# Shared experts of the first half of the tokens beside the second half's scan, and the first half's MLP at twice the pace

## The chip, the cores and the metric

The kernel runs on one core of one Trainium2 chip. The metric is the device time of one execution in microseconds (us). The number that counts is the median of several executions.

## The reference, cut to what matters

One layer for 512 tokens of width 512, in three parts, each added to `x`:

```python
x = x + xattn(layernorm(x), ctx)          # 16 heads, 8192 context rows
u = layernorm(x)
u = u + ssm(rmsnorm(u))                    # mamba: conv, selective scan, gate, out_proj
x = x + u + mlp(rmsnorm(u))                # silu(h w1) * (h w3), times w2; hidden 2048
u = layernorm(x)
logits = u @ router_w                      # 16 experts, top 2, sigmoid gates
moe = sum over the 2 chosen experts of gate * (silu(u wg) * (u wu)) wd      # hidden 512
shared = (silu(u sg) * (u su)) sd          # shared experts, hidden 1024
x = x + moe + shared
```

The scan is `h[t] = exp(delta[t] A) h[t-1] + delta[t] B[t] x[t]` for 1024 channels with 16 states each, and `y[t] = sum over states of C[t] h[t]`.

## The kernel before, in words

Every product of matrices is made in three fp16 products of high and low halves. A framework records the program in the order of the Python code, and a scheduler then puts each engine's instructions into one fixed order; each engine works through its own queue strictly in that order. What the code calls earlier has the higher priority. All loads and stores discussed here are issued from SP's queue.

The attention takes the first 1760 us or so. The tail (function `tail`) does the rest, in two halves of 256 tokens, `s` = 0 and 1:

- `prep(s)` makes the in-projection, convolution and the inputs of the scan. `delta(s, q)` makes the step sizes of a quarter of the channels and the gate input `zs` (products `pd` and `pz`).
- `scan(s, b)` does a block of 128 channels; each quarter `q` has two blocks `b`. A block has four steps of four states. A step is, on ACT, four exponentials into `dA` (L909); on DVE, a product into `hs` (L912), the scan itself (L916) and a product with C (L919); on PE, four fp32 matmuls that add the states up in `py` (L922). There are three buffers `dA` and three `hs`, used in turn. For `s` = 1, ACT also copies the carried states into `hs` (L911). `gate(s, q)` multiplies by `zs` (L928 to L930).
- `outproj(s)` makes the output projection (`px`), updates `u_sb` and makes the normed input `h2` of the MLP.
- `ffn(s, h2, names, pm)` is a generator. It does a gated two-layer product in blocks of 256 hidden channels: 8 blocks for the MLP, 4 for the shared experts. A block loads three pieces of weights of 512 KB into `wpm` (five buffers, L761), makes `pg` and `pu` with 24 matmuls each (L703 to L705), then SiLU on ACT (L966, which needs another activation table than the exponentials), a product on DVE (L967), the fp16 halves `gg` on ACT and DVE (L969, L970), yields, and then does the 12 matmuls of the down product (L709 to L711) into two accumulators. At its end the accumulators are added to `x_sb` on DVE (L978), and it yields once more.
- `ln2(s, xT, fill)` is the norm before the experts with its transposes (L686, L690, L691) and the router products (L1008). It calls `fill` twice, to put other work between.

The quarters of both halves follow each other in one loop (`seq`). From the first block of half 1 on, the loop holds `ml`, the MLP of half 0, and calls it once after the first block of a quarter and once after the second. After the loop come the last gate, `outproj(1)` with one call of `ml`, and the rest of `ml`. Then the buffers of the recurrence are given back (`M.close()`); the expert weights use that space. The MLP of half 1 follows, with `ln2(0)` called inside it; then the shared experts of half 0 (`rs0`) with `ln2(1)` inside; then the choice of experts (top 2, ranks by small products `prk`, slot numbers `sg`), eight indirect DMAs on POOL that scatter the token rows to their experts (L1201), the rest of `rs0`, and the shared experts of half 1. Last, `moe` goes through 16 experts and two spare slots: it gathers the rows of an expert (`xd`, L1208), transposes them, and makes the expert's products. Each expert's weights come in six pieces of 512 KB (`wef`, six buffers, L1089), are split into halves on ACT and DVE (L1094, L1095) and go into `we` (18 buffers) or `wpm`.

Of the kernel before, what the change touches and what calls it, by code (L numbers as in the profile page):

```python
# [632 lines left out]
def tail(tc, a, out, const, scr, ident, x_sb, mlp_d, oT, y_d, xd_d, psums):  # L633
# [16 lines left out]
    def acc(i):  # L650
        if i < 2:
            return ps_s.tile([P, DM], F32, name=f"acc{i}", tag="pss")
        nacc[0] += 1
        if nacc[0] % 3 == 0:
            return ps_o.tile([P, DM], F32, name="acc3", tag="po0")
        return ps_x.tile([P, DM], F32, name="acc4", tag="px")
# [4 lines left out]
    def rsqrt(out_, t, n, tag):  # L661
        nc.scalar.activation(out_, t, AF.Ln)
        nc.scalar.activation(out_, out_, AF.Exp, scale=-0.5)
        w = T.tile([P, n], F32, name=f"nw_{tag}", tag=f"nwt{n}", bufs=2)
        nc.vector.tensor_mul(w, out_, out_)
        nc.vector.tensor_mul(w, w, t)
        nc.vector.tensor_scalar(w, w, -0.5, 1.5, ALU.mult, ALU.add)
        nc.vector.tensor_mul(out_, out_, w)

    def stats(src, n, tag):  # L670
        st = T.tile([P, n, 6], F32, name=f"st_{tag}", tag=f"st{n}", bufs=2)
        mv = T.tile([P, n, 2], F32, name=f"mv_{tag}", tag=f"mv{n}", bufs=2)
        for i in range(n):
            nc.vector.bn_stats(st[:, i, :], src[:, i, :])
            nc.vector.bn_aggr(mv[:, i, :], st[:, i, :])
        return mv

    def small(n, name):
        return T.tile([P, n], F32, name=name, tag=f"sm{n}", bufs=6)
# [20 lines left out]
    def mm_block(ps, w, j, xh, xl, first=True):  # L700
        wr = w.rearrange("p x (b d m) -> p x b d m", b=2, d=NC4)
        for i in range(NC4):
            nc.tensor.matmul(ps, lhsT=wr[:, 0, j, i, :], rhs=xh[:, i, :], start=i == 0, stop=False)  # L703
            nc.tensor.matmul(ps, lhsT=wr[:, 0, j, i, :], rhs=xl[:, i, :], start=False, stop=False)
            nc.tensor.matmul(ps, lhsT=wr[:, 1, j, i, :], rhs=xh[:, i, :], start=False, stop=i == NC4 - 1)  # L705

    def mm_down(ps, xh, xl, w, j, start, stop):
        wh, wl = w[:, 0, j * 512 : j * 512 + 512], w[:, 1, j * 512 : j * 512 + 512]
        nc.tensor.matmul(ps, lhsT=xh, rhs=wh, start=start, stop=False)  # L709
        nc.tensor.matmul(ps, lhsT=xh, rhs=wl, start=False, stop=False)  # L710
        nc.tensor.matmul(ps, lhsT=xl, rhs=wh, start=False, stop=stop)  # L711
# [47 lines left out]
    def wload(n, i):  # L759
        w = F.tile([P, 2, 1024], F16, name="wpm", tag="wpm", bufs=5)  # L760
        nc.sync.dma_start(w, mlp_d[n][i])  # L761
        return w
# [96 lines left out]
    def load_bc(s, k, pool_):  # L859
        bf = bc_d[s].rearrange("(o n) t -> o (n t)", o=1)  # L860
        for nq in range(4):
            x = pool_.tile([P, 4, H], F32, name=f"bc{k}{nq}")
            o = (k * 16 + nq * 4) * H
            nc.sync.dma_start(x.rearrange("p n t -> p (n t)"), bf[:, o : o + 4 * H].to_broadcast((P, 4 * H)))
            BC[s][k, nq] = x
# [59 lines left out]
    def gate(s, q, yT):  # L925
        dl, du, zs, py = dlu.pop((s, q))
        y = m2.tile([P, 2, H], F32, name="y", tag="w2k", bufs=5)
        nc.vector.tensor_mul(y, py, zs)  # L928
        nc.scalar.copy(yT[:, 0, 2 * q : 2 * q + 2, :], y)
        nc.vector.tensor_tensor(yT[:, 1, 2 * q : 2 * q + 2, :], y, yT[:, 0, 2 * q : 2 * q + 2, :], ALU.subtract)  # L930
# [24 lines left out]
    def ffn(s, h2, names, pm):  # L955
        nf = len(mlp_d[names[0]])
        for f2 in range(nf):
            wg, wu, wd = (wload(n, f2) for n in names)
            pg = bank_j([P, 2, H], F32, "pg")
            pu = bank_j([P, 2, H], F32, "pu")  # L960
            for j in range(2):
                mm_block(pg[:, j, :], wg, j, h2[:, 0], h2[:, 1])
            for j in range(2):
                mm_block(pu[:, j, :], wu, j, h2[:, 0], h2[:, 1])
            g = F2.tile([P, 2, H], F32, name="g32", bufs=2)
            nc.scalar.activation(g, pg, AF.Silu, scale=IW)  # L966
            nc.vector.scalar_tensor_tensor(g, pu, IW, g, ALU.mult, ALU.mult)  # L967
            gg = F2.tile([P, 2, 2, H], F16, name="gg", bufs=2)
            nc.scalar.copy(gg[:, 0], g)  # L969
            nc.vector.tensor_tensor(gg[:, 1], g, gg[:, 0], ALU.subtract)  # L970
            yield
            for i in range(2):
                sl = slice(i * P, (i + 1) * P)
                for j in range(2):
                    k = 2 * f2 + j
                    mm_down(pm[i], gg[:, 0, j, sl], gg[:, 1, j, sl], wd, j, k == 0, k == 2 * nf - 1)
        for i in range(2):
            nc.vector.scalar_tensor_tensor(x_sb[:, 2 * s + i], pm[i], IW, x_sb[:, 2 * s + i], ALU.mult, ALU.add)  # L978
        yield
# [5 lines left out]
    nc.vector.scalar_tensor_tensor(rw[:, 1], rwf, WF, rw[:, 0], ALU.mult, ALU.subtract)  # L985
    lg = T.tile([P, 4, 16], F32, name="lg")

    def ln2(s, xT, fill=lambda: None):
        ts_ = slice(2 * s, 2 * s + 2)
        mv = stats(x_sb[:, ts_, :], 2, f"l2{s}")  # L990
        v, r = small(2, f"lv{s}"), small(2, f"lr{s}")
        nc.vector.tensor_scalar(v, mv[:, :, 1], 1e-5, None, ALU.add)
        rsqrt(r, v, 2, f"d{s}")
        h = u_sb[:, ts_]
        for i in range(2):
            nc.vector.tensor_scalar(
                h[:, i], x_sb[:, 2 * s + i], mv[:, i, 0:1], r[:, i : i + 1], ALU.subtract, ALU.mult
            )
        fill()
        transposeT(h, xT[:, 0], xT[:, 1])  # L1000
        fill()
        pl = bank_j([P, 2, 16], F32, "plg")
        for i in range(2):
            sl = slice(i * P, (i + 1) * P)
            n = 0
            for d in range(NC4):
                for x, y in ((0, 0), (0, 1), (1, 0)):
                    nc.tensor.matmul(  # L1008
                        pl[:, i, :], lhsT=xT[:, x, d, sl], rhs=rw[:, y, d, :], start=n == 0, stop=n == 11
                    )  # L1010
                    n += 1
        nc.scalar.activation(lg[:, ts_, :], pl, AF.Copy, scale=IW)

    MLP, RS = ("w1", "w3", "w2"), ("rsg", "rsu", "rsd")

    def h2tile():
        return F2.tile([P, 2, NC4, H], F16, name="h2", bufs=2)
# [27 lines left out]
    h2s = [h2tile() for _ in range(2)]  # L1045
# [2 lines left out]
    xin[1] = const.tile([P, 2, 8, H], F32, name="xin1", tag="big16")[:, 0]  # L1048
    p1 = prep(1)
    yTs = [m3.tile([P, 2, 8, H], F16, name="yT", bufs=2)]  # L1050
    seq = [(s, q) for s in range(2) for q in range(4)]
    ml = None
    for i, (s, q) in enumerate(seq):
        scan(s, 2 * q)
        if s == 0:
            next(p1, None)
        if i:
            gate(*seq[i - 1], yTs[-1])
        if (s, q) == (1, 0):
            outproj(0, yTs[-1], h2s[0])  # L1060
            ml = ffn(0, h2s[0], MLP, [acc(3), acc(3)])
            yTs.append(m3.tile([P, 2, 8, H], F16, name="yT", bufs=2))
        if ml and (s, q) != (1, 0):
            next(ml, None)
        if i + 1 < len(seq):
            if (s, q) == (0, 3):
                for _ in p1:
                    pass
                load_bc(1, 1, m3)
            delta(*seq[i + 1])  # L1070
        scan(s, 2 * q + 1)
        if s == 0:
            next(p1, None)
        if ml:
            next(ml, None)
    gate(1, 3, yTs[-1])
    outproj(1, yTs[-1], h2s[1], lambda: next(ml, None))
    for _ in ml:
        pass
    M.close()  # L1080

    G, g2 = pool(es, "G", "left"), pool(es, "g2", "left")
# [33 lines left out]
    one16 = G.tile([P, 16], F32, name="one16")  # L1116
    nc.gpsimd.memset(one16, 1.0)

    mlp1 = ffn(1, h2s[1], MLP, [acc(0), acc(1)])
    next(mlp1)  # L1120
    xT0 = h2tile()
    ln2(0, xT0, lambda: next(mlp1))
    for _ in mlp1:
        pass
    xT1 = h2tile()
    rs0 = ffn(0, xT0, RS, [acc(3), acc(3)])
    ln2(1, xT1, lambda: next(rs0, None))
    xf = const.tile([P, 4, 2, DM], F16, name="xf", tag="big16")
    nc.scalar.copy(xf[:, :, 0, :], u_sb)
    nc.vector.tensor_tensor(xf[:, :, 1, :], u_sb, xf[:, :, 0, :], ALU.subtract)  # L1130
# [15 lines left out]
        )  # L1146
    oht = G.tile([P, 4, 16], F16, name="oht")
    nc.vector.tensor_add(oht, oh[:, 0], oh[:, 1])
    next(rs0, None)
    prk = bank_j([P, 5, 16], F32, "prk")  # L1150
    for i in range(5):
        n = min(i, 4)
# [118 lines left out]
        moe_down(prev[0], moe_turn(prev[1]), prev[2])  # L1271

    regs = [nc.sync.value_load(oii[0:1, k : k + 1], min_val=0, max_val=15) for k in range(NOV)]
    for _ in rs0:
        pass
    for _ in ffn(1, xT1, RS, [acc(3), acc(3)]):
        pass
    moe(range(16 + MOV), lambda k: expert(k) if k < 16 else overflow(regs[k - 16]))
    total = nc.values_load(oii[0:1, NOV : NOV + 1], min_val=0, max_val=NOV)
# [82 lines left out]
```

## Time and profile before

| | us |
|---|---|
| median of 3 runs | 2606.5 |
| lowest and highest | 2605.04 and 2607.05 |
| profiled execution, its own time | 2611.01 |
| its span, first to last instruction | 2609.3 |
| PE busy | 2383.2 (91%) |
| DVE busy | 2062.4 (79%) |
| ACT busy | 1949.2 (75%) |
| mean DMA rate over the span | 204 GB/s |
| first MLP matmul of half 0 (in the profiled execution) | 2093.2 |
| last L919 of half 1's scan | starts at 2220.3 |
| last expert matmul of the first product (L1225) | starts at 2575.5 |

The profile is of one execution. The table of busy times is an average over very different stages, so the text works with windows of the span, in us from its start. "PEclk" is the granted share of the TensorE clock, "PEld" the loading of weights into the array, "SPq" the queue from which DMAs are issued. A row of waits names the engine and line that waited and what ended its wait. A matmul's duration in a row is longer than the distance to the next one's start, because matmuls overlap.

### The profile page before, as it was taken

Reading aid. Unit: us, or ns where it says so; the run is one execution under the profiler, and the core shown is the slowest. Engines: PE = TensorE matmul, PEld = TensorE weight load, DVE = VectorE, ACT = ScalarE, POOL = GpSimd, SP = SyncE. Lnnn points to the kernel's source line nnn. Section 1 sums busy time; section 2 is a strip of 40 time slices with the busy share of each in tenths; the row PEclk is TensorE's granted clock in tenths of the full one; section 3 lists DMA queues with packets and bytes.
Section 4 is the critical chain, followed back from the end, with each engine's and each line's share of the span. In section 5 each row is a group of like instructions: output and inputs, shape, how many; then the busy total and the mean of one; then the engine's idle time right before and its main releaser. Section 6 shows DMA issues by size and latency. Waiting matters only on the chain. (4 is left out here: it accounts for less than half of the span.)

```text
span 2609.3 us, 54424 instructions
## 1 busy us (share of the span) xinstructions
PE 2383.2 (91%) x21806; PEld 1676.5 (64%) x21806; DVE 2062.4 (79%) x2403; ACT 1949.2 (75%) x3734; POOL 44.3 (2%) x58
## 2 busy tenths in 40 slices
PE   7999899999999999999999998997877688998895
PEld 3555577776677777767777777995665466665442
DVE  6776588888888888878888778997899999533785
ACT  5787788888788888868888888997776476333784
POOL 2000000000000000000000000000000000001001
PEclk9999999999999999999999999999989899999998
DMA  7974677778687778778877655877510222766896
GB/s 270 312 259 138 231 212 231 229 235 241 199 234 235 226 221 251 226 199 228 236 221 213 175 156 148 207 205 192 159 41 25 97 81 82 260 225 217 293 331 208
DMA packets 353688, 531.43 MB, mean 204 GB/s; under 512 B 25107, under 2 KB 218835, under 8 KB 353301
## 3 DMA queue, kind: packets, MB, share of 16 engines
q1 hardware_dynamic: 352148, 523.69, 65.8%
q0 software_dynamic: 1280, 4.20, 0.5%
q8 instruction: 173, 2.83, 0.5%
q14 instruction: 87, 0.70, 0.1%
HBM read 397.68 MB, written 126.94 MB: 201 GB/s over the span
## 5 line engine op out<-in xcount | busy, mean ns | idle before, releaser
L377 DVE TENSOR_TENSOR phl<-p,phl 128x1024 f16<-128x1024 f32 x512 | 626.7, 1225 | 193.2 <-ACT phl L374 181.0
L372 ACT ACTIVATE p<-pss 128x512 f32<-128x512 f32 x1024 | 597.7, 622 | 114.5 <-PE pss L365 42.2
L305 ACT ACTIVATE sf<-psx 128x512 f16<-128x512 f32 x1024 | 558.5, 625 | 70.9 <-PE psx L300 70.1
L364 PE MATMUL pss<-qhh,k 128*128 128x256 f16 x2048 | 481.0, 275 | 14.3 <-ACT phl L374 12.0
L365 PE MATMUL pss<-qlm,kb 128*128 128x256 f16 x2048 | 479.7, 274 | 0.9 <-DMA kb<-k_d 0.9
L313 DVE TENSOR_TENSOR runm<-runm,sf 128x2048 f16<-128x2048 f16 x240 | 292.3, 1219 | 51.7 <-ACT sf L305 51.5
L394 PE MATMUL po<-v,phl 128*128 128x130 f16 x4096 | 322.7, 220 | 3.9 <-DVE oq L407 3.4
L374 ACT ACTIVATE phl<-pss 128x512 f16<-128x512 f32 x512 | 312.8, 611 | 0.0
L394 PEld LDWEIGHTS <-phl 128*128 128x128 f16 x4096 | 271.0, 98 | 61.6 <-issue 14.8
L275 PE MATMUL psv<-wh_v,ctxc 128*128 128x256 f16 x1024 | 282.0, 275 | 7.3 <-ACT wh_v L176 3.2
L276 PE MATMUL psv<-wl_v,ctxc 128*128 128x256 f16 x1024 | 280.8, 274 | 1.2 <-DVE wl_v L177 1.2
L277 PE MATMUL psv<-wh_v,ctxc 128*128 128x256 f16 x1024 | 280.9, 274 | 0.0
L364 PEld LDWEIGHTS <-k 128*128 128x128 f16 x2048 | 200.9, 98 | 66.0 <-issue 20.0
L365 PEld LDWEIGHTS <-kb 128*128 128x128 f16 x2048 | 201.4, 98 | 53.0 <-issue 14.6
L300 PE MATMUL psx<-khl,qh 64*128 64x512 f16 x1024 | 208.9, 386 | 17.6 <-ACT sf L305 12.2
L922 PE MATMUL py<-hs,ident 128*128 128x256 f32 x512 | 144.0, 437 | 73.5 <-DVE hs L919 73.5
L397 PE MATMUL po<-v,phl 128*128 128x65 f16 x4096 | 208.5, 193 | 2.5 <-DVE phl L377 2.5
L251 PE MATMUL psk<-ctxc,wh_k 128*128 128x512 f16 x512 | 198.0, 387 | 9.9 <-ACT ctxc L234 8.1
L376 DVE CAST phl<-p 128x1024 f16<-128x1024 f32 x256 | 176.0, 687 | 32.2 <-ACT p L372 32.0
L252 PE MATMUL psk<-ctxc,wh_k 128*128 128x512 f16 x512 | 196.3, 383 | 0.8 <-DVE ctxc L235 0.7
L253 PE MATMUL psk<-ctxc,wl_k 128*128 128x512 f16 x512 | 196.3, 383 | 0.0
L922 PEld LDWEIGHTS py<-hs,ident 128*128 128x128 f32 x512 | 107.2, 217 | 107.0 <-DVE hs L919 87.0
(304 smaller groups left out, 3774.6 us busy)
## 6 DMA issues: line engine op xcount, KB each, us to landing
v<-v_d SPq DMA_DIRECT2D x128, 520.0 KB
k<-k_d SPq DMA_DIRECT2D x256, 256.0 KB
ctxc<-ctx_d SPq DMA_DIRECT2D x96, 512.0 KB
wef<-in_gu_dram SPq DMA_DIRECT2D x72, 512.0 KB
v_d<-vs SPq DMA_DIRECT2D x128, 260.0 KB
k_d<-khl SPq DMA_DIRECT2D x128, 256.0 KB
kb<-k_d SPq DMA_DIRECT2D x128, 256.0 KB
wpm<-w_d SPq DMA_DIRECT2D x48, 512.0 KB
```

Of the source, the lines that this page charges most:

```text
L275: nc.tensor.matmul(ps[:, t, :], lhsT=ct[i // 2][:, 0, i % 2, sl], rhs=wh[:, i, :], start=i == 0, stop=False)
L276: nc.tensor.matmul(ps[:, t, :], lhsT=ct[i // 2][:, 0, i % 2, sl], rhs=wl[:, i, :], start=False, stop=False)
L277: nc.tensor.matmul(ps[:, t, :], lhsT=ct[i // 2][:, 1, i % 2, sl], rhs=wh[:, i, :], start=False, stop=i == NC4 - 1)
L305: nc.scalar.activation(dst, ps, AF.Copy, scale=1.0 / (8.0 * WS))
L313: nc.vector.tensor_tensor(r, r, sf, ALU.max)
L364: nc.tensor.matmul(ps[:, hh], lhsT=k[:, hh, sl], rhs=qhh[:, hh, qs], start=True, stop=False)
L365: nc.tensor.matmul(ps[:, hh], lhsT=b[:, hh, sl], rhs=qlm[:, hh, qs], start=False, stop=True)
L372: nc.scalar.activation(p32[:, i], pss[i], AF.Exp, scale=sc)
L374: nc.scalar.activation(ph[:, i], pss[i], AF.Exp, scale=sc)
L377: nc.vector.tensor_tensor(pl, p32, ph, ALU.subtract)
L394: nc.tensor.matmul(o, lhsT=ph[:, i, hh, qs], rhs=vv, start=first, stop=False, **kw)
L922: nc.tensor.matmul(py[:, j, :], lhsT=ident, rhs=hs[:, n, 1:], start=k == 0, stop=False)
```

## The change

The MLP of half 0 is called twice at each place where it was called once. Behind it, in the same generator (`half0`), come `ln2(0)` and the shared experts of half 0. What is left of `half0` after the loop and `outproj(1)` is called from `ln2(1)`. The MLP of half 1 runs without anything between, and the shared experts of half 1 are begun before the ranks and finished after the slot numbers.

```diff
-    def ln2(s, xT, fill=lambda: None):
+    def ln2(s, xT):
...
-        fill()
+        yield
         transposeT(h, xT[:, 0], xT[:, 1])
-        fill()
+        yield
...
+    def half0(ml):
+        yield from ml
+        xT0 = h2tile()
+        g = ln2(0, xT0)
+        for _ in g:
+            yield
+        yield from ffn(0, xT0, RS, [acc(3), acc(3)])
+
...
             outproj(0, yTs[-1], h2s[0])
-            ml = ffn(0, h2s[0], MLP, [acc(3), acc(3)])
+            ml = half0(ffn(0, h2s[0], MLP, [acc(3), acc(3)]))
             yTs.append(m3.tile([P, 2, 8, H], F16, name="yT", bufs=2))
         if ml and (s, q) != (1, 0):
+            next(ml, None)
             next(ml, None)
...
         if ml:
             next(ml, None)
+            next(ml, None)
     gate(1, 3, yTs[-1])
     outproj(1, yTs[-1], h2s[1], lambda: next(ml, None))
-    for _ in ml:
-        pass
     M.close()
...
-    mlp1 = ffn(1, h2s[1], MLP, [acc(0), acc(1)])
-    next(mlp1)
-    xT0 = h2tile()
-    ln2(0, xT0, lambda: next(mlp1))
-    for _ in mlp1:
+    for _ in ffn(1, h2s[1], MLP, [acc(0), acc(1)]):
         pass
     xT1 = h2tile()
-    rs0 = ffn(0, xT0, RS, [acc(3), acc(3)])
-    ln2(1, xT1, lambda: next(rs0, None))
+    rs1 = ffn(1, xT1, RS, [acc(3), acc(3)])
+    for _ in ln2(1, xT1):
+        next(ml, None)
+    for _ in ml:
+        pass
...
-    next(rs0, None)
+    next(rs1)
...
-    for _ in rs0:
-        pass
-    for _ in ffn(1, xT1, RS, [acc(3), acc(3)]):
+    for _ in rs1:
         pass
```

## Prediction

> **What bounds the kernel now.** I read the page first: PE is busy 91% and DVE 79% of the span, which says little, because the stages differ. So I cut the end of the span at events of the timeline: first MLP matmul of the first half, last scan step, last MLP drain of the second half, first gather of expert rows, first expert matmul.
>
> ```profile
> core 0: us, PE busy (x) PEld busy (x) DVE busy (x) ACT busy (x) POOL busy (x), PEclk, DMA share, GB/s
> 2093.00:2222.00 129.00, 104.22 (x627) 79.43 (x625) 125.16 (x103) 86.69 (x167) 4.78 (x5) 0.97 0.27 86
> 2222.00:2322.00 100.00, 95.93 (x692) 65.90 (x691) 43.46 (x75) 36.08 (x50) 0.00 (x0) 0.98 0.77 268
> 2322.00:2387.00 65.00, 60.83 (x483) 43.26 (x481) 25.21 (x66) 21.46 (x30) 7.85 (x8) 1.00 0.53 180
> 2387.00:2402.00 15.00, 6.63 (x35) 4.70 (x36) 3.81 (x5) 3.81 (x5) 0.00 (x0) 0.66 0.67 233
> 2402.00:2610.00 208.00, 164.75 (x939) 79.40 (x936) 149.69 (x157) 134.46 (x163) 8.51 (x8) 0.93 0.79 277
> ```
>
> The scan stage (quarters 1 to 3 of the second half, 24 scan steps) is DVE's: 125.2 of 129 us. The next 100 us (outproj, MLP of half 1, norm of half 0) are PE's. The 65 us after it look like PE too, but the chain of router, ranks and eight scatters runs through them, 2322.2 to 2387.2, and PE only fills it with the shared experts. Then PE stands still. The waits of that stretch say why, first PE's, then the SP queue's own (us in total, times, longest):
>
> ```profile
> PE pu L703 <- DMA wpm<-rsu_d: 8.8, 1, 8.8
> ```
>
> ```profile
> SPq L1208 <- DMA xd_d<-xf,sg: 14.5, 1, 14.5
> ```
>
> The last shared-expert weight load stands on SP behind the gather `xd`, which waits for the scatters.
>
> Next the timeline, for the prices: columns are start, duration, engine, line.
>
> ```profile
> 2106.18 4.48 DVE L916 TENSOR_TENSOR_SCAN hs<-dA,hs 128x1028 f32<-128x1028 f32 x2
> 2110.58 2.33 DVE L919 TENSOR_TENSOR hs<-hs,bc 128x1024 f32<-128x1024 f32 x2
> 2112.83 2.35 DVE L912 TENSOR_TENSOR hs<-bc,du 128x1024 f32<-128x1024 f32 x2
> ...
> 2145.41 0.67 DVE L967 SCALAR_TENSOR_TENSOR g<-pu,g 128x512 f32<-128x512 f32 x1
> ...
> 2191.11 0.27 PE L703 MATMUL pg<-h,wpm 128*128 128x256 f16 x1
> 2191.22 0.27 PE L704 MATMUL pg<-h,wpm 128*128 128x256 f16 x1
> ...
> 2210.29 3.73 PE L922 MATMUL py<-hs,ident 128*128 128x256 f32 x16 [2.25 <-DVE hs L919]
> ```
>
> By starts, a step costs DVE 2.2+1.14+1.14 = 4.5 us, an ffn block 0.6+0.6 = 1.2. On PE a 128x256 f16 matmul issues every 0.108, a 128x512 every 0.215 (2214.07, 2214.28, 2214.50 at L709 to L711), one step's `py` (L922) takes 1.68.
>
> **The change, part by part.** Work is neither added nor removed; the ffn blocks change place. I take the order of instructions of both built programs and these prices.
>
> *MLP of half 0 at twice the pace.* One block is 48x0.108 + 12x0.215 = 7.8 us of PE. Before, a quarter holds about two: 15.5 + `py` 2x(4x1.68+0.42) = 14.2 + `pd`,`pz` 2.9 = 32.6 of PE, beside DVE's 8x4.5 + 2x1.2 + 3.6 (delta, gate) = 42; the trace shows 40 (2141.0 to 2181.1, first step of quarter 2 to that of quarter 3). After, quarters 1 and 2 hold four each: PE 31.1+14.2+2.9 = 48.2, DVE 36+4.8+3.6 = 44.4. Both exceed 40, so these two quarters lose at least 16.
>
> They lose more, because the order on PE is now: two blocks, one after the other, then `py` of up to three steps in one piece, and `pd`,`pz` of the next quarter behind two blocks. The ring of `hs` has three buffers; L912 on DVE waits until `py` has read one. And on DVE L967 of a block stands before the next steps and waits for `pu`. I walked the order from 2102, each instruction at the price of its row:
> - quarter 1: PE, done with `pg` of block 3 at 2128.9, waits until 2132.9 for block 2's cast `gg`, which stands on ACT behind two carry copies; block 2's down product, `pu` of block 3, `pd`,`pz` and the `py` of three steps are queued behind that wait. So DVE waits 4.9 for `pu` of block 3 (2133.9 to 2138.8), then 0.7 for the cast and 1.9 for `py`; delta of quarter 2 comes late. First step of quarter 2: 2152.4 against 2141.0, +11.4 (2.4 of it two more blocks on DVE).
> - quarter 2: DVE waits 3.3 and 6.0 for `pu` of blocks 5 and 7, about 3 in casts and `py`. First step of quarter 3: 2210.1 against 2181.1, +29.0.
>
> *Norm and router of half 0, beside quarter 3.* DVE: two drains (L978) 1.2, two bn_stats 1.2, small ones 0.9, two L996 0.9, two L691 1.2: 5.4. PE: 8 transposes 1.2, 24 router matmuls 0.7; `py` of one step stands behind them and waits for L690/L691, hidden, since DVE has two other steps meanwhile. ACT has room (86.7 of 129).
>
> *Shared experts of half 0.* Only block 0 fits: in the built order PE starts block 1 in full, and block 2, after the last `py`. The last scan step ends at 2252.3 in the walk, 2221.5 in the trace: **+30.8**. Their 12 loads (6.3 MB) move on SP from behind MLP 1 to before the output projection's loads; DMA is busy 27% there and the five `wpm` buffers turn as before: nothing. Uncovered it would be 6.3 MB at 268 GB/s, 23. POOL gets nothing new. The expert weights start when the scan's buffers are released, so 31 later too; before, they had filled their buffers by 2300.8, 80 ahead of the first gather, and that covers it.
>
> *After the scan.* Outproj now stands behind `pu` of blocks 1 and 2: second `px` ends 25.8 after the scan, before 16.7: +9.1. Norm of half 0 leaves MLP 1's stretch: 1.2+0.7 = −1.9. MLP 1's drain ends at 2360 instead of 2322.2; sum **+7.2**.
>
> *Router chain.* The chain from drain to slot numbers took 29.8 (2322.2 to 2352.0). Now there is one shared block in it instead of two, so 26: **−3.8**. Eight scatters up to the gather: 35.2, kept.
>
> *Gather to first expert matmul.* 15.1 before (2387.2 to 2402.3), with the wait for `rsu`. In the new order on SP all loads of the shared experts, and three expert loads, stand ahead of `xd`, so PE is through 4 blocks (31 us) and free: landing about 3.5, transposes 1.0, copy 1.1: 6, **−9.1**.
>
> *Experts.* They keep PE 165 of 208 us and DMA 79%. The weight stream restarts with the gather as before (SP is in order), three of 108 pieces further. At 1.6 to 2 us each that is −5 at most, 0 where PE paces it: I take **−2**.
>
> Sum: 30.8+7.2−3.8−9.1−2 = +23.1. On the profiled execution (span 2609.3, its time 2611.0) that gives 2634; that execution is 4.5 above the median 2606.5, so on the median 2629.6.
>
> **Two rules against these rows.** The Trainium skill, "Perfetto Trace Analysis", Optimization Strategy: when the most contended engine changes over time, interleaving those regimes may help. This is that case: DVE 97% before 2222, PE 96% after. By the rule PE loses 31+2 us of work late and DVE gains 5+5 early: −23, 2583. By the rows a quarter needs 48.2 of PE, so the regime flips: +23. The same page, Identifying the Most-Contended Engine, judges room on TensorE by LDWEIGHTS busy, not matmul busy. That is 79.4/129 = 62%, so 38% of a 40 us quarter, 15, is free, and two more blocks (15.5) fit: quarters 1 and 2 then stay near DVE's 44, +8 in place of +29, and the sum is +2. But issue intervals give 32.6 of 40 taken: 7 free. I go with the intervals, because a 128x512 matmul holds PE 0.215 for a load of 0.098 (L709's rows), and LDWEIGHTS time doesn't see the rest.
>
> **Rivals.**
> - *Only work counts, no waits (15%).* Quarters 1 and 2 cost PE's 48.2 each, quarter 3 +6.6: scan +23 instead of +31, median 2622. For it: engines run ahead over buffers. Against it: three `hs`, two `g32`, strict order.
> - *Not slower: the experts fall to PE's floor (7%).* Place: the 18 experts. An expert is 36x0.215+1.0 = 8.75 of PE; 18 make 157.5, and with the 27 us tail 185 instead of 207. If the earlier pieces keep ACT from waiting for weights (20.8 us in the waits of this stretch), up to −22 falls due in place of −2: 2609.5 with the scan as walked, 2602 with the smaller scan loss. It decides from 20 us on. Against it: PE's idle there is mostly `xk` (14.8), in the order itself.
> - *Heavier (15%).* Waits I priced at 0.1 are longer, or PE's grant falls with the gaps (0.66 in 2387 to 2402): scan +45, median 2645.
> - *The change does less than it says*: already in the likeliest case, one shared block of four inside the scan.
>
> **Chances.** Likeliest 63%, 2620 to 2640. The measurement of this kernel can tell about 0.2% (5 us) from no change. Faster needs floor and small loss together: 0.04; within 0.2%: 0.06; slower: 0.90. Low end 2608 (floor), high end 2653 (heavier, with a longer scatter chain).
>
> **What would show it.** Right: four blocks per quarter with DVE idle at L967 for `pu`, a last L919 near 2252 (2237 or less: the waits are wrong); block 1 to 3 of the shared experts after it; no wait for `rsu`; gather near 2421; PE idle some 15 us before it. Wrong: DVE without gaps in quarters 1 and 2, or experts in under 195 us.

## The result, and the profile after

The changed kernel takes 2637.5 us (median of 4, 2635.6 to 2638.4) against 2605.8 (4 runs, 2600.9 to 2607.1) for the kernel before on the same chip: a ratio of 1.0122, 95% interval 1.0109 to 1.0135. It is slower. Its profiled execution has a span of 2635.3 and a time of its own of 2637.0. The forecast was 2630, between 2608 and 2653.

The spans of the two profiles differ by 26.0, the medians by 31.7, because the profiled execution of before was 5.2 above the median here and that of after 0.5 below. I cut the changed profile at the same events as in the prediction (first MLP product of the first half, end of the scan, last MLP drain of the second half, first gather of expert rows, first expert matmul; the columns are those of the prediction's table):

```profile
2094.90:2258.80 163.90, 132.26 (x821) 98.20 (x818) 135.24 (x124) 89.91 (x176) 0.73 (x5) 0.94 0.29 94
2258.80:2369.50 110.70, 102.99 (x723) 70.54 (x724) 40.34 (x67) 34.71 (x46) 0.00 (x0) 0.98 0.74 261
2369.50:2426.50 57.00, 38.58 (x290) 26.47 (x288) 28.54 (x66) 20.17 (x26) 8.36 (x8) 0.88 0.40 139
2426.50:2431.20 4.70, 1.06 (x9) 0.80 (x10) 0.00 (x0) 1.01 (x1) 0.00 (x0) 0.50 0.82 272
2431.20:2635.30 204.10, 163.86 (x928) 79.31 (x928) 143.96 (x150) 131.25 (x159) 8.54 (x8) 0.93 0.79 280
```

The first row is the one to read. In the kernel before, the scan stage was full of VectorE work (cut exactly, 124.7 of 128.3 us). Now it lasts 163.9 and no engine fills it: DVE 135.2, PE 132.3. Of the 35.6 us more, 10.5 are more work on DVE and 25.1 are time in which DVE stands. The second row is longer too, 110.7 where the kernel before has 100.6; the three after it give back 8.1, 10.4 and 2.8.

What does DVE wait for? The waits of the stage, DVE only (us in total, times, longest), first in the kernel before, 3.5 in all, then in the changed one, 28.0:

```profile
DVE hs L912 <- PE py L922: 1.5, 2, 0.9
DVE gg L970 <- ACT gg L969: 1.5, 1, 1.5
DVE hs L916 <- ACT dA L909: 0.5, 1, 0.5
```

```profile
DVE g L967 <- PE pu L705: 17.7, 3, 7.6
DVE gg L970 <- ACT gg L969: 5.7, 6, 1.5
DVE hs L912 <- PE py L922: 4.1, 2, 2.0
DVE hs L916 <- ACT dA L909: 0.5, 1, 0.5
```

The timeline places the three big ones, and the last scan step (the bracket is the idle time before the instruction and what ended it):

```profile
2143.33 0.69 DVE L967 SCALAR_TENSOR_TENSOR g<-pu,g 128x512 f32<-128x512 f32 x1 [7.56 <-PE pu L705]
...
2175.21 0.69 DVE L967 SCALAR_TENSOR_TENSOR g<-pu,g 128x512 f32<-128x512 f32 x1 [4.07 <-PE pu L705]
...
2203.47 0.69 DVE L967 SCALAR_TENSOR_TENSOR g<-pu,g 128x512 f32<-128x512 f32 x1 [6.10 <-PE pu L705]
...
2257.59 1.22 DVE L919 TENSOR_TENSOR hs<-hs,bc 128x1024 f32<-128x1024 f32 x1
```

Each is the second block of a pair: DVE's next steps of the recurrence stand behind L967, and L967 behind PE's two blocks in a row.

At the gather, PE's waits from the last MLP drain to the first expert matmul no longer hold a shared-expert weight; ahead of the experts PE waits for the gather itself, the longest of these waits (the second longest, in the router chain, is for the norm), and SP's queue goes straight from expert weights to the gather (SP's rows):

```profile
PE pxd L1220 <- DMA xd<-xd_d: 10.3, 1, 10.3
PE pt L686 <- DVE u_sb L996: 5.6, 1, 5.6
```

```profile
2408.10 6.67 SPq L1098 DMA_DIRECT2D wef<-in_gu_dram  x3
2426.46 1.28 SPq L1216 DMA_DIRECT2D xd<-xd_d  x3
```

### The profile page after: what moved, and what is told of

The parts are those of the page before. It is cut to its first block, busy times and chain, and to the rows that moved or that the text cites. A ratio compares the mean times of both kernels' runs of the same rounds, so it can differ in the third digit from the quotient of the medians.

```text
span 2635.3 us, 54406 instructions
## 1 busy us (share of the span) xinstructions
PE 2388.7 (91%) x21806; PEld 1680.3 (64%) x21806; DVE 2062.0 (78%) x2403; ACT 1943.0 (74%) x3729; POOL 40.5 (2%) x58
## 5 line engine op out<-in xcount | busy, mean ns | idle before, releaser
L364 PE MATMUL pss<-qhh,k 128*128 128x256 f16 x2048 | 480.9, 275 | 15.3 <-ACT phl L374 11.4
L394 PEld LDWEIGHTS <-phl 128*128 128x128 f16 x4096 | 272.1, 98 | 62.0 <-issue 14.8
L376 DVE CAST phl<-p 128x1024 f16<-128x1024 f32 x256 | 176.0, 687 | 31.8 <-ACT p L372 31.6
```

The costliest lines, as they stand in the source:

```text
L364: nc.tensor.matmul(ps[:, hh], lhsT=k[:, hh, sl], rhs=qhh[:, hh, qs], start=True, stop=False)
L394: nc.tensor.matmul(o, lhsT=ph[:, i, hh, qs], rhs=vv, start=first, stop=False, **kw)
```

## The experiments

"Scan stage" is the time from the first MLP product of the first half to the end of the last L919, taken from each profile; DVE work and PE busy are those of a window cut there.

| kernel | ratio to before (95%) | scan stage | DVE work | DVE idle | PE busy |
|---|---|---|---|---|---|
| before | 1 | 128.3 | 124.7 | 3.6 | 103.5 |
| after | 1.0122 (1.0109 to 1.0135) | 163.9 | 135.2 | 28.7 | 132.3 |
| after, second time | 1.0138 (1.0102 to 1.0174) | 164.4 | 135.2 | 29.2 | 134.5 |
| pace alone | 1.0091 (1.0070 to 1.0113) | 159.4 | 130.2 | 29.2 | 130.1 |
| all but the pace | 1.0078 (1.0064 to 1.0092) | 126.6 | 124.5 | 2.1 | 103.2 |
| after, calls spread | 1.0053 (1.0033 to 1.0073) | 155.9 | 135.9 | 20.0 | 130.6 |
| after, milder pace | 1.0035 (1.0022 to 1.0049) | 148.4 | 133.7 | 14.8 | 121.7 |
| after, cast on DVE | 1.0111 (1.0096 to 1.0125) | 163.9 | 138.7 | 25.2 | 134.5 |
| after, shared experts left out | 1.0031 (1.0021 to 1.0042) | 162.1 | 133.9 | 28.2 | 130.9 |
| before, shared experts left out | 0.9927 (0.9903 to 0.9951) | – | – | – | – |
| before, gathers from POOL | 0.9993 (0.9981 to 1.0005) | – | – | – | – |
| before, two shared blocks in the tail | 1.0005 (0.9995 to 1.0015) | – | – | – | – |
| the same, ahead of the test | 0.9993 (0.9983 to 1.0002) | – | – | – | – |
| the same, with more buffers | 1.0003 (0.9995 to 1.0011) | – | – | – | – |

### The changed kernel again

> The changed kernel unaltered, on the chip of these runs, as their reference: 2633 to 2640 us, with the last scan step ending 160 to 167 us after the first product of the MLP, if the delay of the recurrence is a property of its order; a scan end that varies by more than 5 us would mean that the comparisons of the stage between kernels are good to no better than that.

2637.0 us. The scan stage is 164.4, 163.9 in the first profile: the delay belongs to the order of instructions. In the seven profiles at the old pace the stage is 126.6 to 128.9, so a difference of 2 us between two profiles says nothing.

### The pace alone, and all but the pace

The kernel before with the doubled calls of the MLP and nothing else:

```diff
         if ml and (s, q) != (1, 0):
+            next(ml, None)
             next(ml, None)
...
         if ml:
             next(ml, None)
+            next(ml, None)
```

> The kernel before with only the double pace of the first half's MLP; norm, router products and shared experts of the first half stay where they were. My theory (the pace costs: TensorE needs 48 us in a quarter of 40, and the pairs of blocks stand ahead of py): the first step of quarter 3 comes 30 to 36 us later than in the kernel before, as in the changed kernel, some 12 us of it are given back after the scan because the last MLP blocks are out of it, median 2620 to 2632. Rival (norm and shared experts beside the scan are what costs, the pace is free): within 5 us of before.

2630.6 us, ratio 1.0091, inside the theory's range. The scan stage is 159.4, with the same three waits for `pu` as in the changed kernel (16.7 us in all). So the pace by itself makes 31 of the 35.6 us. The other 4.5 come when norm, router products and the first shared block stand beside the scan as well; they put 5 us more work on DVE.

The counterpart is the changed kernel with these two lines taken out:

> The changed kernel at the old pace: one block at each place in place of two, all else as the change has it, so that the MLP of the first half just ends with the recurrence, and its norm and all four shared blocks come behind the second half's MLP, ahead of the ranks. The other part of the change alone. Theory (the delay of the recurrence comes from the pace and from nothing else in the change): the last scan step ends 126 to 131 us after the first product of the MLP, as before; two more shared blocks stand in the router chain, which takes 40 to 48 us from drain to slot numbers in place of 29.6; the gathers then find TensorE free, as in the changed kernel, -10; the sum is 0 to +8, 2606 to 2616 us. Rival (the longer generator moves instructions of the recurrence too): the scan ends 135 us or more after it, and the run takes over 2618.

2623.5 us, ratio 1.0078. Half of the expectation held: the scan stage is 126.6, so at the old pace nothing else in the change delays the recurrence; norm and shared experts then come after it. The total missed, and the stage is the router chain. It takes 62.0 us from drain to slot numbers, before 29.6. Its window:

```profile
2318.00:2380.00 62.00, 50.76 (x396) 36.13 (x395) 24.89 (x78) 15.10 (x25) 0.00 (x0) 0.86 0.41 128
```

I had expected 40 to 48, for four blocks. The group of `pu` matmuls counts 40 a line, 8 a block: five blocks, as the first shared block of the second half stands ahead of the ranks too. PE also waits 10.8 in that window for the two norms. Each half of the change alone makes the kernel slower.

### Shared experts left out, before and after

Both kernels leave the shared experts of the first half of the tokens out of the output, so they price these blocks where they stand. In the kernel before:

```diff
-    rs0 = ffn(0, xT0, RS, [acc(3), acc(3)])
+    rs0 = iter(())
```

> The kernel before with the shared experts of the first half left out altogether (31 us of TensorE, so the output lacks them). It tells what moving them can bring at most in the late stage. My theory: the late stage is bound by the chain of router, ranks and scatters, which gives back what the changed kernel's late stage gave back: 5 in the chain, 3 in the scatters, 10 at the gather, so about -18, median 2585 to 2592. Rival (the late stage is bound by TensorE): -31 or more, median 2575 or less.

2589.6 us: 17.7 less than before. The chain bounds: drain to slot numbers is 19.4, and from the gather to the first expert matmul it is 5.2 instead of 15.1. In the changed kernel:

```diff
         for _ in g:
             yield
-        yield from ffn(0, xT0, RS, [acc(3), acc(3)])
```

> The changed kernel without the shared experts of the first half (left out; norm and router products of that half stay where the change puts them). Theory: where the change runs them, the shared experts are not covered. Blocks 1 to 3 lie between the scan's end and the second half's products, and ahead of the router chain, so leaving them out gives back about the 10 us by which that stretch grew, and the scan, whose pace stays doubled, keeps its 34 us of delay less what block 0 cost in it. 2616 to 2624 us. Rival (they run free beside the recurrence, and only the pace costs): 2633 to 2640. Second rival (they also hold the recurrence back, several blocks of them): below 2610.

2613.1 us, just below the range, and 23.9 less than the changed kernel on the same chip. So the four blocks cost 24 us where the change puts them, and 18 where they stood before: **they were not hidden by the move**. That they cost more than before isn't shown, as the interval of the ratio before is wide (0.9903 to 0.9951, or 13 to 25 us). The scan stage keeps 162.1 of 163.9, too small a difference to price block 0. What can be placed lies after the scan: from its end to the second `px` 9.4 us instead of 26.7, and MLP 1's stretch 79.6 instead of 84.0. My 10 us was wrong because I had compared with before's 16.8: that still holds work of the first half's MLP, 7.4 us of it by this run (about one block's 7.8), which the doubled pace has done by then.

### Pairs, spread calls, and a milder pace

All calls of the changed kernel, but one at a time: one in the middle of each block of channels as well, none twice.

```diff
-    def scan(s, b):
+    def scan(s, b, mid=lambda: None):
...
+            if nq == 1:
+                mid()
...
-        scan(s, 2 * q)
+        scan(s, 2 * q, lambda: next(ml, None) if ml else None)
...
-            next(ml, None)
...
-        scan(s, 2 * q + 1)
+        scan(s, 2 * q + 1, lambda: next(ml, None) if ml else None)
...
-            next(ml, None)
```

> The changed kernel, with the four calls of a quarter spread one by one: two of them in the middle of a scan block instead of two together at its end. Same pace, same work in a quarter. If the waits come from two blocks standing together ahead of py, the scan ends 10 to 16 us earlier than in the changed kernel and the median is 2622 to 2628. If only the work of TensorE in a quarter counts, nothing changes: 2635 to 2640. If order is everything, the scan loses only its added VectorE work, 9 us, and the median is about 2611.

2621.8 us: spreading the same blocks gives back 8 us of the scan stage, less than the 10 to 16 expected, though the total came out just below that forecast's range. The long waits for `pu` are gone from DVE's waits, which are now many small ones:

```profile
DVE gg L972 <- ACT gg L971: 8.4, 8, 1.6
DVE g L969 <- ACT g L968: 5.5, 4, 2.1
DVE hs L912 <- PE py L922: 4.8, 2, 2.4
```

The stage stays 28 longer than before, so neither "only the work counts" nor "order is everything" holds alone. Next, three single blocks a quarter, two calls instead of one in `outproj(1)`, and what is left over after the slot numbers:

```diff
-        scan(s, 2 * q)
+        scan(s, 2 * q, lambda: next(ml, None) if ml else None)
...
-            next(ml, None)
...
-        scan(s, 2 * q + 1)
+        scan(s, 2 * q + 1, lambda: next(ml, None) if ml and q == 0 else None)
...
-            next(ml, None)
...
-    outproj(1, yTs[-1], h2s[1], lambda: next(ml, None))
+    outproj(1, yTs[-1], h2s[1], lambda: [next(ml, None) for _ in range(2)])
...
+    for _ in ml:
+        pass
     for _ in rs1:
...
```

> The changed kernel at a milder pace: three single blocks a quarter in place of four in pairs (the first one after the first half of a block's state products, then after the gate, then after the second block), and four of the calls that are left over put as pairs into the second half's output projection. The shared experts of the first half that are still over by then run after the router's slot numbers, as before. Theory (a quarter is overloaded when TensorE's work for it passes VectorE's 40 us; three blocks and the recurrence's own products make about 40): the scan ends 128 to 140 us after the first product of the MLP, and the run takes 2603 to 2615 us. Rival (any pace above two a quarter delays the recurrence in proportion, half of what the spread pairs cost): 2614 to 2622.

2617.2 us (2615.5 by the ratio). The theory said 128 to 140 for the scan stage and got 148.4 (in an execution of 2609.5, the fastest of the seven), so it missed. The rival's direction holds, not its size: the stage is 20 longer than before, where half of what the spread pairs cost would be 14. Three blocks a quarter, spread, don't come free either. DVE was full before the change (3.6 us idle), so its added work (9.0 us) is paid, and its waits for casts and `py` come on top, though PE is busy only 121.7 of 148.4.

### The cast on VectorE

In quarter 1 PE waits 3.6 us for a cast on ACT. I thought it stood behind ACT's carry copies, and that this queue was the part of the scan's delay that my walk had missed, and moved the casts of the first half's blocks:

```diff
-            nc.scalar.copy(gg[:, 0], g)
+            (nc.scalar.copy if s else nc.vector.tensor_copy)(gg[:, 0], g)
```

> The changed kernel with the fp16 cast of the first half's blocks on VectorE in place of ScalarE, so that TensorE no longer waits for a cast behind ScalarE's carry copies. Theory (these waits, 10.5 us in five places, and the halved pace of TensorE after the longest are the part of the scan's delay that the walk had missed): VectorE gets some 5 us more work in the stage, TensorE's waits for the cast fall below 3 us, and the last scan step ends 155 to 161 us after the first product of the MLP in place of 164; the run takes 2629 to 2636 us, as the casts of the shared blocks in the router chain then cost VectorE some more. Rival (the number of blocks a quarter sets the pace, whatever a block waits for): 163 to 168, and 2636 to 2644.

2633.0 us lies in the theory's range, but the scan stage is 163.9, where the theory wanted 155 to 161, and PE's wait for the cast is still there, on another engine:

```profile
DVE g L967 <- PE pu L705: 18.1, 3, 8.3
...
PE acc L709 <- DVE gg L969: 11.6, 4, 3.8
```

The ratio's interval overlaps those of the changed kernel. The theory falls, and the changed kernel's own rows say why: the cast comes 0.03 us after L967 ends, and L967 stands behind a scan step on DVE, which has no idle time there.

```profile
2131.16 2.29 DVE L916 TENSOR_TENSOR_SCAN hs<-dA,hs 128x1028 f32<-128x1028 f32 x1
2133.37 0.67 DVE L967 SCALAR_TENSOR_TENSOR g<-pu,g 128x512 f32<-128x512 f32 x1
2134.07 0.62 ACT L969 CAST gg<-g 128x512 f16<-128x512 f32 x1 [0.38 <-DVE g L967]
```

So moving the cast between these two queues could not shorten the wait; what a shorter wait would be worth, this run doesn't tell.

### The gather and the tail

The gathers `xd` of the kernel before, issued from POOL instead of SP, so that the last shared-expert weights need not stand behind them:

```diff
-        nc.sync.dma_start(xd, xd_d[k * P : (k + 1) * P, :].rearrange("t (x d m) -> t x d m", x=2, d=NC4))
+        nc.gpsimd.dma_start(xd, xd_d[k * P : (k + 1) * P, :].rearrange("t (x d m) -> t x d m", x=2, d=NC4))
```

> The kernel before with the gathers of expert rows issued from GpSimd's queue instead of SP's, so that the last weight loads of the shared experts and the expert weights don't stand behind the wait for the scatters. If the stall of 15 us ahead of the first expert matmul is SP's order and the experts are paced by their weights: -10 to -20, median 2586 to 2596. If the scatters end it anyway and TensorE paces the experts: 0 to -9, median 2597 to 2606. If issuing from GpSimd costs more per gather than it frees, slower than before.

2606.3 us, ratio 0.9993: no change, a miss. PE's wait for `rsu` went, and a wait of 10.5 for the gather took its place. The first gather is issued at 2394.9 instead of 2387.2. Of these 7.7 us, 2.4 were there at the first scatter, 2.7 come from the eight scatters (34.0 from the first to the last instead of 31.3), and 2.6 lie between the last scatter and the gather; the first expert matmul comes at 2403.8 instead of 2402.4. Weight loads are now in flight beside the last scatters; that this is what slows them was not tried apart.

If the chain bounds and PE is idle in the last 23 us, two of the four blocks could move there (`ffn` gets the range of its blocks):

```diff
-    rs0 = ffn(0, xT0, RS, [acc(3), acc(3)])
+    rs0 = ffn(0, xT0, RS, [acc(3), acc(3)], range(2))
...
+    for _ in ffn(0, xT0, RS, [acc(3), acc(3)], range(2, 4)):
+        pass
-    for i in range(4):
+    for i in (2, 3, 0, 1):
```

> The kernel before with the other half of its shared experts moved out of the router chain instead: of the four blocks of the first half, two stay in it, and two run after the last expert's products, beside the last gathers of the output, and the output tiles of the second half are finished first. Theory (the chain to the gathers is what bounds, and TensorE is idle in the tail): the chain gets 7 to 10 us shorter, the tail takes at most 3 more, 2596 to 2603 us. Rival (the tail's first tile waits for the two blocks, 16 us of products): 2606 to 2614.

2607.9 us, ratio 1.0005. The first part came: drain to slot numbers 20.1 instead of 29.6, and the last expert product starts at 2567.9 instead of 2581.8. The tail took it back, and the time is in the rival's range. Between the last expert product and the stretch of the two blocks, the last 28.3 us, lies a gap of 8.1. In it PE waits 8.2 for weights, whose loads stand behind the test for overflowed experts. So I put the blocks ahead of that test, and then gave the output gathers four more buffers:

```diff
+    for _ in ffn(0, xT0, RS, [acc(3), acc(3)], range(2, 4)):
+        pass
     total = nc.values_load(oii[0:1, NOV : NOV + 1], min_val=0, max_val=NOV)
...
-            yg = g2.tile([P, DM], F32, name="yg", tag="yo", bufs=4)
+            yg = g2.tile([P, 2 * DM], F32, name="yg", tag="wef", bufs=6)[:, :DM] if i > 1 else g2.tile([P, DM], F32, name="yg", tag="yo", bufs=4)
```

> As the kernel with two shared blocks of the first half in the tail, but with these two blocks ahead of the test for overflowed experts, so that their weights can load beside the last experts. Theory (in that run the experts ended 13 us earlier than before, and the tail lost it again because the weights of its two blocks were loaded only after the test, which left TensorE idle for 8 us and then at half its pace): the two blocks follow the last expert within 2 us at full pace, and the run takes 2596 to 2604 us. Rival (the tail is bounded by the gathers of the output and the adds that now stand behind the blocks on VectorE): 2604 to 2610.

> The same, and the first four gathers of the output use the idle buffers of the expert weights, so that all eight can be in flight while the two blocks run. Theory (gathers five to eight wait for the adds, which stand behind the blocks): 3 to 6 us less than without it, 2592 to 2600 us. Rival (the blocks' own end sets the tail): equal to it within 1 us.

2603.2 and 2606.4 us, ratios 0.9993 and 1.0003: no difference from before that these runs can show. The first lies in its theory's range, but that range reached almost to no change; the added buffers were to bring 3 to 6 us and brought none that shows. The gap is gone, as PE is busy 15.4 of 17.0 us after the last expert, but the first output gather waits for the test, which now comes after the blocks (POOL's row, of the run without the added buffers):

```profile
2585.83 0.98 POOL L1287 DMA_INDIRECT yg<-y_d,sg  x1 [210.56 <-ACTq L1282]
```

L1282 is the test, and it was ACT's part of it, behind the blocks in ACT's queue, that released POOL, 14.9 us after the last expert product; in the kernel before, the first output gather waits for the test too, but comes 5.2 us after that product. From the last expert product's end (2571.0) to the end of the span it is 34 us, in the kernel before 23. No version of these beats the kernel before.

## Why the prediction was right, and which term was too small

The sign and the mechanism held; the median is 7.5 above the forecast and inside the range. By the prediction's steps, measured as lengths between the same events in both profiles (the rows of quarters 2 and 3 are parts of the scan stage and not in the sum):

| step | predicted | measured |
|---|---|---|
| quarter 2 starts later | +11.4 | +14.8 |
| quarter 3 starts later | +29.0 | +34.3 |
| scan stage | +30.8 | +35.6 |
| scan end to second `px` | +9.1 | +9.9 |
| second `px` to MLP 1's drain | −1.9 | +0.2 |
| drain to slot numbers | −3.8 | −5.4 |
| slot numbers to gather | 0 | −2.7 |
| gather to first expert matmul | −9.1 | −10.4 |
| experts and tail | −2 | −2.8 |
| sum | +23.1 | +24.4 |

The sum is right to 1.3, and that close by luck, since two errors cancel: the scan cost 4.8 more than forecast, and the later steps gave back 3.5 more. Another 1.7 of the 26.0 lies ahead of the change: the first MLP product of the first half comes at 2094.9 instead of 2093.2, and over the profiles of this study that event, with the same code ahead of it, lies anywhere from 2089.7 to 2096.3. And the medians are 31.7 apart, 8.6 more than the sum: 5.7 of that is how far the two profiled executions lie from their medians, and no profile shows where it arises.

The mis-sized term is the wait for `pu` of a pair's second block: 17.7 us in three waits, where the walk had 4.9 + 3.3 + 6.0 = 14.2. The first wait accounts for 2.7 of the 3.5, 7.6 for 4.9, and the trace shows what the walk left out. A window of quarter 1 in the changed kernel (PEclk, the column after POOL, is 0.50), and PE's rows at its start:

```profile
2134.70:2140.00 5.30, 5.26 (x14) 2.10 (x15) 1.07 (x2) 0.00 (x0) 0.00 (x0) 0.50 0.00 0
```

```profile
2134.74 0.61 PE L709 MATMUL acc<-wpm,gg 128*128 128x512 f16 x1 [3.60 <-ACT gg L969]
2135.14 0.64 PE L710 MATMUL acc<-wpm,gg 128*128 128x512 f16 x1
2135.57 0.64 PE L709 MATMUL acc<-wpm,gg 128*128 128x512 f16 x1
```

The walk had the wait of 4 us for the cast, but priced what comes after it at full pace. After it the granted clock is 0.50 for 5.3 us, and the 128x512 matmuls start every 0.43 instead of 0.215: twelve of them lose 2.5 us, all ahead of the `pu` that DVE waits for. Two other profiles have the same instructions at this place. In the changed kernel without shared experts (first two rows) the grant after the cast is 1.00, and DVE waits 4.9, just the walk's price; in the changed kernel's second run (last two rows) it falls to 0.50 from 2132.7 to 2136.0, and DVE waits 6.6:

```profile
2130.13 0.39 PE L709 MATMUL acc<-wpm,gg 128*128 128x512 f16 x1 [3.13 <-ACT gg L969]
2136.06 0.69 DVE L967 SCALAR_TENSOR_TENSOR g<-pu,g 128x512 f32<-128x512 f32 x1 [4.90 <-PE pu L705]
2132.01 0.39 PE L709 MATMUL acc<-wpm,gg 128*128 128x512 f16 x1 [3.12 <-ACT gg L969]
2139.62 0.69 DVE L967 SCALAR_TENSOR_TENSOR g<-pu,g 128x512 f32<-128x512 f32 x1 [6.59 <-PE pu L705]
```

So the walk's order was right here, and the grant makes the difference. The Trainium skill, "TensorE: Matmul & The Clock Gate", Part 1, has the rule that belongs to this: after an idle window of about 3.4 us TensorE falls back to half its clock, until it has been busy for about as long. The changed kernel's row agrees (3.60 us idle), and with the walk's wait of 4 us the rule would have put the 2.5 us into it. But 3.13 us idle left the grant whole and 3.12 did not, so near this length the wait alone doesn't tell what follows. That PE's wait itself, and not something else at that moment, sets the clock, was not tried apart.

The walk also read the wait for the cast wrongly: it put the cast behind two carry copies on ACT, but the rows under the cast on VectorE show L967 on DVE ahead of it. The length came out about right all the same (4.0 for 3.6).

**The two rules.** The Trainium skill, "Perfetto Trace Analysis", Optimization Strategy, with its interleaving of stages, gave 2583; here each half of the change alone made the kernel slower. Room judged by LDWEIGHTS time (same page, Identifying the Most-Contended Engine) gave +2 in the sum; the quarter with two more blocks did not fit, and even one more block a quarter cost (the milder pace: +20 us of scan stage). The issue intervals were the right measure of PE, but not the bound either: in the changed scan stage PE is busy 132 of 164. The larger part of the delay, 25.1 of 35.6 us, is DVE standing, and its waits are for products and casts of the filler and for `py`: two queues, each in order, that wait for each other.

**The rivals.** "Only work counts, no waits" put 23 into the scan. It is out: the scan cost 35.6, PE stands for 31.6 us of the changed stage, and the same blocks called one at a time took 8 less. "Not slower" needed experts under 195; they took 204.1. "Heavier" priced the scan at +45, and its grant falling with gaps did happen, for 5 us where it hurts; the stage came between the likeliest case and it. "Does less than it says" held as the likeliest case had it: one shared block inside the scan, and the blocks 1 to 3 after it, two of them before `px`.

**The signs named.** DVE idle at L967 for `pu`: yes, three times. Last L919 near 2252: 2258.8 is its end. No wait for `rsu`: yes. Gather near 2421: 2426.5. PE idle some 15 us before it: less, 10.3 up to the transposes of `xd` at 2429.0, so 7.8 before the gather's issue.

## What to carry to other kernels

Before filling one engine's idle time from another stage, write out what the busy engine must do for the filler: here each block put two instructions on a VectorE that was 97% full, and the first of them stood behind a product on TensorE, with the next steps of the recurrence behind it. Two fillers in a row can make the wait for the second one nearly as long as one block's work (4.1 to 7.6 us, for a block of 7.8), so single calls between the bound engine's steps are cheaper (here by 8 us of 36), but not free. A block moved out of a chain that bounds is worth something only if its new place has slack on every queue that it touches; leaving the blocks out in both places (18 us against 24) shows in two runs whether the move hid them.

## What was not expected of the hardware

- After a wait of 3.60 us, TensorE ran at a granted clock of 0.50 for 5.3 us, in the middle of a stage whose mean grant is 0.94. The same wait of 3.1 us was followed by a grant of 1.00 in one profile and by 0.50 within 1 us in another.
- Moving the gathers to POOL took away a wait of 8.8 us behind SP's queue and changed the time by less than 0.2%: PE waited 10.5 us for the gather instead.
- The first MLP product, with the same code ahead of it, came within a range of 6.6 us over the profiles, which is more than several of the steps above. Stages had to be compared from an event behind it.
